# A transformer-like chain of eight stages on one core: norms moved to other engines, three MLP parts and some clearing moved in time

## The chip, the cores and the metric

The kernel runs on one core of a Trainium2 chip. A core has a matrix engine (TensorE, in the profile PE, with its weight loads listed apart as PEld) and three engines for the rest: VectorE (DVE), ScalarE (ACT) and GpSimd (POOL). Every engine takes its instructions in a fixed order and waits on semaphores for the others. SyncE (SP) issues most plain DMAs, and POOL issues the gathers and scatters whose addresses are data. The metric is the device time of one execution in microseconds (us). The kernel is measured over several runs and the median counts; the profile comes from one further execution.

## The reference, cut to what matters

There are 8192 tokens of 128 features, 32 sequences of 256. Four layers follow one another, and each has an attention half and a feed-forward half, all of one form:

```
h = _layernorm(x) * (1 + ca) + sa
x = x + ga * attention(h, ...)
h = _layernorm(x) * (1 + cb) + sb
x = x + gb * feed_forward(h, ...)
```

The halves that the change touches are these.

```
# layer 0, feed-forward: a shared MLP and 8 experts, two chosen per token
shared = new_gelu(xf @ Wfc_s + bfc_s) @ Wproj_s + bproj_s
probs = softmax(xf @ Wr);  topk_p, topk_i = top_k(probs, 2)      # renormalized
routed = sum_e gate[:, e] * (new_gelu(xf @ Wfc[e] + bfc[e]) @ Wproj[e] + bproj[e])
return shared + routed

# layer 1, feed-forward: 8 experts with a capacity of 512 token copies
logits = relu(x @ rw1 + rb1) @ rw2 + rb2
vals, ids = top_k(logits, 2);  probs = softmax(vals)
pos = cumsum(one_hot(ids)) - 1;  keep = pos < CAP
disp[ids, pos] += x * keep                                        # 8 x 512 rows
eo = relu(disp @ ew1 + eb1) @ ew2 + eb2
y = eo[ids, pos] * probs * keep

# layer 3, attention: 16 heads of 8, keys and values from a latent of 32
q = x @ Wq + bq
latent = x @ Wl + bl
k = latent @ Wk + bk;  v = latent @ Wv + bv
out = (softmax(q k^T * 8 ** -0.5) v) @ Wo + bo
```

The layer norm has no weights here; it needs the mean, the variance and 1 / sqrt(variance + 1e-5) of each token. Between the two routed halves lies the attention of layer 1 (called hale in the code), and behind the latent attention an MLP with four-bit rounding of its operands (fp4_mlp).

## The kernel before

The residual stream x stays in on-chip memory as 16 blocks, each 128 features by 512 tokens. The eight halves run one after the other. In the profiled execution the first routing (`dense_moe`) takes 1107 to 1376 us, its 39 expert blocks 1376 to 1682, `hale` 1682 to 3731, the second routing (`capacity_moe`) 3731 to 4000 and its experts to 4085, `phase_attention` 4085 to 4790, `head_moe` to 5545, `latent_attention` 5545 to 6400 and what is left of `fp4_mlp` to 6648.

**Order.** Each stage fills an agenda: `put(t, f)` places a piece of work in slot t, and then all slots are gone through in order. Within a slot, work is done in the order in which it was put there. The instructions of an engine are issued in this order; a flag (`strict`) keeps them in program order where a scheduler could change it. So an agenda slot fixes a place in the queue of every engine that the work uses, and a waiting instruction holds back everything behind it on its engine.

**First routing.** Token block b has T = 4b: statistics in slot T, norm in T + 1, the modulated h in T + 3, router logits and the choice of two in T + 5, slot numbers and the scatter of token rows to per-expert regions in DRAM in T + 10 (POOL, eight scatters of 128 rows), gates in T + 13, and the shared MLP in T + 24 to T + 27 (`shared_part`, L1117: four matmuls to 512 hidden features, each with a gelu on ACT, then one for the bias and four for the outputs, and the residual on DVE). In slot 72 the totals are formed, and 39 expert blocks follow, four slots apart: `block_fetch` gathers weights and 4 x 128 rows by POOL, `block_turn` transposes them, `block_hidden` and `block_out` multiply, and the results go to DRAM. Block j has its first matmuls in slot 4 (23 + j) = 92 + 4j and its last in slot 99 + 4j.

**hale.** At its start POOL waits for the last expert rows, clears the tiles for maxima (`mts`), for values (`vzb`, `vzl`) and for key states (`kvs`), and then runs eight gathers per token block (`gather_rows`), which DVE sums up, weighted, into the residual of the routed experts. These are side works from slot 32 b - 62 on for token block b, in this stage's own count.

**Second routing.** Again T = 4b: `norm_stats` (L417) leaves the turned rows in PSUM and mean and variance in SBUF; `norm_apply` (L435) makes the root and the normed rows; `norm_out` modulates; `router_hidden` has four matmuls with relus, `router_sums` the logits, `router_choice` the choice of two (`choose`, L1051, with the running counts `both` and `past`), and `capacity_slots` positions and scatters. The root is taken on DVE by `newton_parts` (L960): two integer operations and four Newton steps, which is 14 operations of 128x4. In the trace they stand between those of the choice of two.

**Latent attention.** Per token block there are 16 score groups, eight for each of two sequences; each has maxima (`max_step`, DVE reduces a score tile), scores again with the maxima taken off, exponentials (`exp_step`, ACT) and weighted values. `before(b)` puts the preparation of a block around its first slot: statistics at -14 (`norm_rows`, L446, copies the turned rows to SBUF and takes statistics), the root and the normed rows at -13 and -12 (`norm_place`, L462: DVE), h at -10, latent at -8, q at -6, keys at -4 (`keys`, L1548), values at -2. The keys are kept twice, masked for even and odd heads; ACT writes the four masked copies straight from the score buffer S in PSUM, with the bias and a row of ones (for the maxima) added by the same instruction. The front of the last stage runs ahead in here too, one token block behind: `mlp_norm` and the rest of `mlp_front`, four slots from its norm to its h. Only token block 15's front is left for the last stage.

Of the kernel before, what the change touches and what calls it, by code (L numbers as in the profile page):

```python
# [24 lines left out]
AF = mybir.ActivationFunctionType  # L25
ALU = mybir.AluOpType
# [4 lines left out]
P = 128  # L31
NSEQ, SEQ = 32, 256
NB = 16
TB = 512
# [106 lines left out]


def rows(v):

    v = np.asarray(v, np.float32).reshape(1, -1)
    return np.broadcast_to(v, (P, v.shape[1]))
# [29 lines left out]
def packs(d):  # L176
# [91 lines left out]
    k.add("Wl", g["Wl"])  # L268
    k.add("Wk", spread(g["Wk"]))
    k.add("Wo", gathered(g["Wo"]))  # L270
    k.add("Wv", np.concatenate([g["Wv"], g["bv"][None]], 0))
    k.add("bq", spread(g["bq"][None])[0].T)
    k.add("kb", key_bias(g["bk"]))
    k.add("bo", col(g["bo"]))
# [41 lines left out]
class Program:  # L316
# [129 lines left out]
    def norm_rows(self, src, small=None, tag="ln_xn"):  # L446
# [13 lines left out]
        return xn, mv, v  # L460

    def norm_place(self, xn, mv, v):  # L462

        rs = self.wk("ln_rs", (P, 4))
        yield from self.newton_parts(rs, v, "ln")
        for n in range(4):
            self.nc.vector.tensor_scalar(
                xn[:, n, :], xn[:, n, :], mv[:, n, 0:1], rs[:, n : n + 1], ALU.subtract, ALU.mult
            )
        yield  # L470
# [7 lines left out]

    def norm_newton(self, mv, v, r):


        pool = self.nc.gpsimd
        t = self.wk("ln_t", (P, 4))
        pool.tensor_tensor(t, r, r, ALU.mult)
        pool.tensor_tensor(t, t, v, ALU.mult)
        pool.tensor_scalar(t, t, -0.5, 1.5, ALU.mult, ALU.add)
        pool.tensor_tensor(r, r, t, ALU.mult)
        shift = self.wk("ln_m", (P, 4))
        pool.tensor_tensor(shift, mv[:, :, 0], r, ALU.mult)
        pool.tensor_scalar(shift, shift, -1.0, None, ALU.mult)  # L490
        return r, shift

    def norm_scale(self, xn, r, shift):
# [482 lines left out]
    def dense_moe(self, w):  # L976
# [8 lines left out]
        with ExitStack() as ctx:  # L985
# [19 lines left out]
            def put(t, f, *args):  # L1005
                agenda.setdefault(t, []).append((f, args))

            for b in range(NB):
                a = {"b": b}
                T = 4 * b  # L1010
                put(T + 1, lambda a: a.update(xn=self.norm_apply(*a["st"])), a)
                put(T + 0, lambda a: a.update(st=self.norm_stats(self.x[a["b"]])), a)
                put(T + 3, lambda a: a.update(h=self.norm_out(a["xn"], self.ada_mods(0, 1, a["b"]), "h")), a)
                put(T + 5, self.route_logits, m, a)
                put(T + 10, self.route_slots, m, a)
                put(T + 13, self.route_gates, m, a)
                for i in range(4):
                    put(T + 24 + i, self.shared_part, m, a, i)
            end = 4 * NB + 8
# [528 lines left out]
    def keys(self, h, w, bias):  # L1548
# [14 lines left out]
        return k4  # L1563


    def hale(self, w):
        nc, c = self.nc, self.c
        BF = mybir.dt.bfloat16
        with ExitStack() as ctx:
# [8 lines left out]
            self.vzl = [keep.tile([P, 4, 16, 32], F, name=f"vzl{t}") for t in (0, 1)]  # L1578
            for t in self.mts + self.vzb + self.vzl:
                nc.gpsimd.memset(t, 0.0)  # L1580
            for t in self.vzb + self.vzl:
                nc.gpsimd.memset(t[:, :, :, 8:16], 1.0)
            self.identb = wk("identb", (P, P), BF)
# [4 lines left out]
            self.kvs = wk("kvs", (P, 5, SEQ))  # L1588
            nc.gpsimd.memset(self.kvs, 0.0)
            self.kt = wk("kt", (P, 5, P))  # L1590
# [19 lines left out]
            self.gather = None  # L1610

    def hale_slots(self, w):

# [6 lines left out]

        tiles = {}
        for q in range(2 * NB):
            b, s = divmod(q, 2)
# [402 lines left out]
    def capacity_moe(self, w):  # L2026
# [3 lines left out]
        with ExitStack() as ctx:  # L2030
# [6 lines left out]
            self.pools(ctx, {"tp": 2, "hid": 3, "o": 1, "s": 2}, zero=1, ht=4, dk=4, hid=3, eo=3, h=3)  # L2037
            self.strict = self.newton = True
            zero = self.wk("zero", (P, 8 * P))
# [14 lines left out]
            for b in range(NB):  # L2054
                a = {"b": b}
                T = 4 * b
                put(T + 1, lambda a: a.update(xn=self.norm_apply(*a["st"])), a)
                put(T + 0, lambda a: a.update(st=self.norm_stats(self.x[a["b"]])), a)
                put(T + 3, lambda a: a.update(h=self.norm_out(a["xn"], self.ada_mods(1, 1, a["b"]), "h")), a)
                put(T + 5, self.router_hidden, m, a, 0)  # L2060
                put(T + 6, self.router_hidden, m, a, 1)
                put(T + 8, self.router_sums, m, a)
                put(T + 10, self.router_choice, m, a)
                put(T + 12, self.capacity_slots, m, a)
# [9 lines left out]
            for t in sorted(agenda):  # L2074
                for f, args in agenda[t]:
                    f(*args)
            self.strict = self.newton = False
            self.gather = {"eo": eo, "rows": 8 * CAP}
# [390 lines left out]
    def latent_attention(self, w):  # L2469
        nc, c = self.nc, self.c  # L2470
        self.mlp_start()
        with ExitStack() as ctx:
# [7 lines left out]
            def before(b, tiles):  # L2480
                t = tiles[b] = {"vz": self.vzs[4 * (b % 2) : 4 * (b % 2) + 4]}

                def head():
                    t["st"] = self.norm_rows(self.x[b])
                    t["norm"] = self.norm_place(*t["st"])

# [16 lines left out]
                def k():  # L2503
                    t["k4"] = self.keys(t["lat"][:32, :], w.Wk, w.kb)

# [100 lines left out]
    def mlp_norm(self, a):  # L2606
        a["st"] = self.norm_rows(self.x[a["b"]], tag="fx")
        a["norm"] = self.norm_place(*a["st"])

# [212 lines left out]
```

## Time and profile before

| | us |
|---|---|
| median of 10 runs | 6653.41 |
| lowest and highest run | 6627.98, 6663.11 |
| the profiled execution's own time | 6649.74 |
| span from its first to its last instruction | 6647.3 |
| PE busy in the span | 5819.3 (88%) |
| DVE busy | 4316.2 (65%) |
| ACT busy | 3493.0 (53%) |
| POOL busy | 2660.8 (40%) |
| mean granted clock of TensorE | 0.936 |

The busy shares are means over eight stages with different limits, so the page of the whole kernel says little about one stage. The table of stretches gives busy time and granted clock for a chosen window, and the timeline gives single instructions with the idle time ahead of each and what ended it. In a line of the timeline stand: start, duration, engine, source line, operation, the tiles written and read, the shape, the count, and in brackets the idle time with its releaser. Line L304 is a helper through which DVE's instructions of the later stages are issued, and L392, L396 and L399 are helpers for matmuls, transposes and activations; there one goes by the tile names.

### The profile page before, as it was taken

To read this page: it belongs to the slowest core of one execution; us is meant where nothing else is said; L and a number is where in the kernel's file an instruction comes from. 1 tells how busy PE (TensorE), PEld (TensorE's weight loads), DVE (VectorE), ACT (ScalarE), POOL (GpSimd) and SP (SyncE) were. 2 spreads that over 40 slices of the span, in tenths; PEclk is the share of its full clock that TensorE was granted. 3 is DMA by queue.
4 is the path that set the end of the run, shared out by engine and by line. 5 is a ranking of instruction groups with operands and counts; after the bars stand their busy time and mean duration, and the time that the engine had idled before them with its cause. 6 is when DMAs were issued, how large, how long until landed. Compare 5 with 4: busy or idle time off the path is not lost. (4 is left out here: it accounts for less than half of the span.)

```text
span 6647.3 us, 132969 instructions
## 1 busy us (share of the span) xinstructions
PE 5819.3 (88%) x54369; PEld 3292.5 (50%) x54369; DVE 4316.2 (65%) x9937; ACT 3493.0 (53%) x5026; POOL 2660.8 (40%) x2882
## 2 busy tenths in 40 slices
PE   6788886989899999999999767999799998999986
PEld 4555554456455555555555434555422223444443
DVE  4777776611466666666665553888677774777779
ACT  5888884333344444444444332444388885554532
POOL 3555553565444544544544452444245452000000
PEclk8999997899899999999999778999899998998989
DMA  1110110134000000000000101111044341000011
GB/s 62 42 42 29 42 42 34 37 114 131 22 6 5 7 6 5 7 6 5 7 2 2 47 1 38 27 28 28 29 96 92 90 93 41 17 18 18 17 33 30
DMA packets 175877, 232.19 MB, mean 35 GB/s; under 512 B 46567, under 2 KB 95967, under 8 KB 175010
## 3 DMA queue, kind: packets, MB, share of 16 engines
q1 hardware_dynamic: 124880, 126.50, 7.5%
q0 software_dynamic: 26992, 56.62, 3.4%
q10 hardware_dynamic: 23394, 40.58, 1.6%
q8 instruction: 426, 6.98, 0.4%
q14 instruction: 185, 1.52, 0.1%
HBM read 88.22 MB, written 74.97 MB: 25 GB/s over the span
## 5 line engine op out<-in xcount | busy, mean ns | idle before, releaser
L304 DVE TENSOR_REDUCE mt<-S 128x4 f32<-128x1024 f32 (+2 forms) x768 | 756.0, 999 | 514.0 <-PE S L392 510.8
L1438 ACT ACTIVATE E<-S 128x1024 f32<-128x1024 f32 x448 | 458.9, 1024 | 546.2 <-PE S L392 507.0
L875 DVE TENSOR_TENSOR_SCAN hs<-decay,dB 128x512 f32<-128x512 f32 x512 | 583.0, 1204 | 91.8 <-PE dB L392 77.2
L399 ACT ACTIVATE hid<-S,bigw 128x1024 f32<-128x1024 f32 x512 | 537.4, 1112 | 121.2 <-PE S L392 121.0
L1912 POOL TENSOR_SCALAR_AFFINE_SELECT E<-E 128x1024 f32<-128x1024 f32 x320 | 349.4, 1094 | 583.8 <-ACT E L1911 583.3
L304 DVE TENSOR_TENSOR E<-S,cst 128x1024 f32<-128x1024 f32 x320 | 391.3, 1223 | 288.9 <-PE S L392 287.3
L392 PE MATMUL S<-qa,kx 32*128 32x256 f32 x4096 | 538.5, 382 | 34.4 <-DVE mt L304 34.0
L392 PE MATMUL S<-kx,q 32*128 32x512 f32 (+1 forms) x2048 | 527.8, 610 | 17.0 <-ACT kx L1556 16.1
L1911 ACT COPY E<-S 128x1024 f32<-128x1024 f32 x320 | 323.6, 1011 | 326.0 <-PE S L392 314.1
L2459 POOL TENSOR_TENSOR acc<-acc,ye 128x512 f32<-128x512 f32 x256 | 344.7, 1347 | 359.0 <-DVE ye L304 316.3
L392 PEld LDWEIGHTS S<-qa,kx 32*128 32x128 f32 x4096 | 340.7, 190 | 142.7 <-DVE mt L304 106.7
L392 PE MATMUL S<-qG,f 32*128 32x512 f32 x2560 | 367.6, 644 | 47.5 <-DVE E L304 47.5
L392 PE MATMUL S<-hm,bigw 32*128 32x512 f32 x2048 | 336.8, 649 | 25.2 <-ACT hid L399 25.2
L399 ACT ACTIVATE hsT<-hT 128x1024 f32<-128x1024 f32 x256 | 260.9, 1019 | 157.1 <-PE hT L396 156.2
L399 ACT ACTIVATE decay<-dl,A 128x510 f32<-128x510 f32 x512 | 339.1, 714 | 0.0
L396 PE MATMUL hT<-cst,hs 128*128 128x128 f32 x2048 | 295.7, 290 | 22.6 <-ACT hsT L399 21.5
L392 PE MATMUL po<-hid,bigw 128*32 128x512 f32 x2048 | 277.9, 615 | 30.1 <-DVE ye L304 30.1
L392 PE MATMUL po<-E,vz 128*32 128x256 f32 x4096 | 294.2, 372 | 0.3 <-ACT oc L1458 0.2
L1787 ACT ACTIVATE E<-S 128x768 f32<-128x768 f32 (+1 forms) x192 | 169.2, 881 | 237.9 <-PE S L392 237.9
L304 DVE TENSOR_TENSOR ye<-po,gb 128x512 f32<-128x512 f32 x256 | 176.0, 687 | 173.4 <-PE po L392 106.4
L392 PE MATMUL po<-E,vzl 128*32 128x128 f32 x8192 | 276.7, 276 | 0.0
L396 PEld LDWEIGHTS hT<-cst,hs 128*128 128x128 f32 x2048 | 235.1, 147 | 82.5 <-ACT hsT L399 65.0
(530 smaller groups left out, 12931.6 us busy)
## 6 DMA issues: line engine op xcount, KB each, us to landing
gb<-gT SPq DMA_DIRECT2D x256, 256.0 KB
regions<-zeros ACTq DMA_DIRECT2D x16, 2048.0 KB
rx<-far SPq DMA_DIRECT2D x64, 256.0 KB
expert_rows<-eo SPq DMA_DIRECT2D x39, 256.0 KB
xin<-in_x SPq DMA_DIRECT2D x16, 256.0 KB
out<-out SPq DMA_DIRECT2D x16, 256.0 KB
xTd<-xT SPq DMA_DIRECT2D x15, 256.0 KB
xT<-xTd SPq DMA_DIRECT2D x15, 256.0 KB
```

The source lines that it names most:

```text
L304: return lambda *args, **kw: self.tc.keep_in_program_order(op(*args, **kw))
L392: return self.tc.keep_in_program_order(self.nc.tensor.matmul(out, lhsT, rhs, start=start, stop=stop, **kw))
L396: return self.tc.keep_in_program_order(self.nc.tensor.transpose(out, in_, self.c.ident[:k, :k]))
L399: ins = self.nc.scalar.activation(*args, **kw)
L875: nc.vector.tensor_tensor_scan(hs[:, :, n], decay, dB[:, :, n], 0.0, ALU.mult, ALU.add)
L1438: nc.scalar.activation(e, src, AF.Exp, scale=scale)
L1787: nc.scalar.activation(e, src, AF.Exp, scale=1.0 / math.sqrt(8))
L1911: nc.scalar.copy(e, src)
L1912: nc.gpsimd.affine_select(e, e, [[0, 8], [1, P]], ALU.is_ge, 0.0, base=0, channel_multiplier=-1)
L2459: nc.gpsimd.tensor_tensor(a["acc"], a["acc"], ye, ALU.add)
```

## The change

It has four parts.

1. In the first routing the shared MLP of token blocks 9, 10 and 11 leaves its slots (60 to 71) and goes to slots 252 to 263, behind the last expert block, whose last outputs are in slot 251.
2. At hale's start the clearing leaves its place ahead of the stage and becomes a side work (`hale_zeros`) in slot -47, behind the eight gathers of the first token block (-62 to -50).
3. In the second routing the root is taken by ACT (logarithm, then the exponential of minus half of it) with one Newton step of four operations on DVE, and ACT instead of DVE writes the normed rows, from PSUM, with scale and bias. A table that holds both functions is loaded at the stage's start.
4. In latent attention, and in the part of the last stage's front that runs there, the root comes from ACT in the same way, and POOL does the variance's offset, the Newton step and the normed rows (`norm_apart`). The keys' bias becomes a 33rd row of the key weights; ACT copies the key tile to SBUF once, and POOL makes the masked copies from it, in two multiplications by the mask (`masked_keys`).

```diff
+    def norm_turned(self, ps, mv, v):
+        nc = self.nc
+        rs, shift = self.wk("ln_rs", (P, 4)), self.wk("ln_m", (P, 4))
+        self.rsqrt(rs, v, "ln")
+        nc.vector.scalar_tensor_tensor(shift, mv[:, :, 0], -1.0, rs, ALU.mult, ALU.mult)
+        xn = self.wk("ln_xn", (P, 4, P))
+        for n in range(4):
+            self.act(xn[:, n, :], ps[:, n, :], AF.Identity, bias=shift[:, n : n + 1], scale=rs[:, n : n + 1])
+        return xn
...
+    def norm_apart(self, xn, mv, v):
+        r = self.norm_roots(v)
+        yield
+        r, _ = self.norm_newton(mv, v, r, False)
+        for n in range(4):
+            self.nc.gpsimd.tensor_scalar(
+                xn[:, n, :], xn[:, n, :], mv[:, n, 0:1], r[:, n : n + 1], ALU.subtract, ALU.mult
+            )
+        yield
...
+                last = 4 * (8 + blocks + b + 7) if 9 <= b < 12 else T + 24
                 for i in range(4):
-                    put(T + 24 + i, self.shared_part, m, a, i)
+                    put(last + i, self.shared_part, m, a, i)
...
+    def masked_keys(self, lat, w):
+        pk = self.ps("S", (P, 2, TB))
+        for x in (0, 1):
+            self.mm(pk[:, x, :], w[:, x, :], lat)
+        both = self.wk("kk", (P, 2, TB))
+        self.nc.scalar.copy(both, pk)
+        k4 = self.wk("kx", (P, 2, 2, TB))
+        for x in (0, 1):
+            self.nc.gpsimd.tensor_tensor(
+                k4[:, x],
+                both[:, x, :].unsqueeze(1).to_broadcast([P, 2, TB]),
+                self.c.half.unsqueeze(2).to_broadcast([P, 2, TB]),
+                ALU.mult,
+            )
+        return k4
...
-            for t in self.mts + self.vzb + self.vzl:
-                nc.gpsimd.memset(t, 0.0)
-            for t in self.vzb + self.vzl:
-                nc.gpsimd.memset(t[:, :, :, 8:16], 1.0)
...
-            nc.gpsimd.memset(self.kvs, 0.0)
...
+        put(side, -47, self.hale_zeros)
...
-            self.strict = self.newton = True
+            self.strict = True
+            self.use_ln_exp()
...
-                put(T + 1, lambda a: a.update(xn=self.norm_apply(*a["st"])), a)
+                put(T + 1, lambda a: a.update(xn=self.norm_turned(*a["st"])), a)
...
-                    t["st"] = self.norm_rows(self.x[b])
-                    t["norm"] = self.norm_place(*t["st"])
+                    t["st"] = self.norm_rows(self.x[b], nc.gpsimd)
+                    t["norm"] = self.norm_apart(*t["st"])
...
-                    t["k4"] = self.keys(t["lat"][:32, :], w.Wk, w.kb)
+                    t["k4"] = self.masked_keys(t["lat"], w.Wk)
...
-        a["st"] = self.norm_rows(self.x[a["b"]], tag="fx")
-        a["norm"] = self.norm_place(*a["st"])
+        a["st"] = self.norm_rows(self.x[a["b"]], self.nc.gpsimd, "fx")
+        a["norm"] = self.norm_apart(*a["st"])
```

## The prediction

> **What bounds the kernel now.** I read the table of stretches first (columns: us; busy us and instructions of PE, PEld, DVE, ACT, POOL; granted clock; DMA share; GB/s), cut at the stages that the change touches.
>
> ```profile
> 1107.00:1376.00 269.00, 218.04 (x718) 114.65 (x719) 147.31 (x920) 71.03 (x127) 147.44 (x162) 0.80 0.13 42
> 1376.00:1682.00 306.00, 305.02 (x1715) 213.66 (x1716) 53.19 (x77) 107.24 (x156) 174.90 (x176) 1.00 0.46 127
> ...
> 3731.00:4000.00 269.00, 168.00 (x583) 84.76 (x583) 150.90 (x1029) 83.94 (x146) 131.31 (x150) 0.71 0.12 34
> ...
> 5640.00:6400.00 760.00, 700.27 (x5574) 355.24 (x5573) 554.26 (x1375) 387.18 (x488) 6.20 (x12) 0.94 0.06 19
> 6400.00:6648.00 248.00, 179.23 (x627) 102.09 (x625) 223.03 (x295) 69.91 (x134) 0.00 (x0) 0.89 0.11 32
> ```
>
> First routing (row 1) and second routing (row 3) have no full engine: they are chains of latencies. The expert blocks (row 2) are PE's alone, 305 of 306 us. Latent attention (row 4) is nearly PE's: 60 us idle, and a clock of 0.94. The last stage (row 5) is DVE's, 223 of 248. POOL is empty in rows 4 and 5.
>
> Then the timeline at the end of the first routing, PE only:
>
> ```profile
> 1329.36 3.60 PE L392 MATMUL hid<-h,w 128*128 128x512 f32 x8
> 1332.89 1.12 PE L392 MATMUL o<-gT,w 9*128 9x512 f32 x2
> 1333.94 3.70 PE L392 MATMUL o<-hid,w 128*128 128x512 f32 x8
> 1337.47 3.60 PE L392 MATMUL hid<-h,w 128*128 128x512 f32 x8
> ...
> 1364.84 2.08 PE L392 MATMUL hid<-h,w 128*128 128x512 f32 x2 [15.43 <-ACT hid L399]
> ...
> 1374.27 0.60 PE L396 MATMUL tp<-cst,dk 128*128 128x128 f32 x4
> ```
>
> One shared part costs PE 1337.47 − 1329.36 = 8.1 us. The last one sits in a standstill of 15.4 us while POOL issues the first blocks' gathers; block 0 begins at 1374.27. The next stage's start, on all engines:
>
> ```profile
> 1680.88 0.69 DVE L1257 COPY eo<-o 128x512 f32<-128x512 f32 x1 [4.12 <-PE o L392]
> ...
> 1684.01 1.32 POOL L1580 MEMSET mt<- 128x256 f32 x4 [21.41 <-DMA expert_rows<-eo]
> ...
> 1693.37 1.01 POOL L1266 DMA_INDIRECT got<-expert_rows,back  x1 [0.16 <-issue]
> ...
> 1706.10 0.88 DVE L539 SCALAR_TENSOR_TENSOR x<-tp,mods,x 128x256 f32<-128x256 f32 x2 [0.57 <-PE tp L396]
> ```
>
> The gathers start 12.5 us after the last block: 3.1 us until its rows land, 9.4 us of clearing. The second routing's DVE, within one block's choice:
>
> ```profile
> 3875.53 1.36 DVE L441 TENSOR_SCALAR ln_xn<-tp,ln_mv,ln_rs 128x128 f32<-128x128 f32 x4
> 3876.83 0.19 DVE L588 TENSOR_TENSOR rt_o<-rt_t,rt_f 128x32 f32<-128x32 f32 x1
> ```
>
> The next block's norm (1.36 us) stands between two links of this block's top-2 chain. Last, latent attention: a timeline, another, the table of waits, and a tile of phase attention.
>
> ```profile
> 6136.16 0.88 DVE L304 SCALAR_TENSOR_TENSOR x<-y,mods,x 128x256 f32<-128x256 f32 x2 [1.26 <-ACT y L2524]
> ...
> 6138.14 1.11 DVE L304 TENSOR_SCALAR ln_xn<-ln_xn,ln_mv,ln_rs 128x128 f32<-128x128 f32 x4
> 6139.17 1.22 DVE L304 TENSOR_REDUCE mt<-S 128x4 f32<-128x1024 f32 x1
> ...
> 6140.44 1.48 PE L392 MATMUL S<-qa,kx 32*128 32x256 f32 x8 [1.39 <-DVE mt L304]
> ```
>
> ```profile
> 5652.64 0.92 PE L392 MATMUL S<-kx,q 32*128 32x512 f32 x2 [1.07 <-ACT kx L1556]
> ```
>
> ```profile
> PE S L392 <- DVE mt L304: 30.3, 37, 1.4
> ...
> PE S L392 <- ACT kx L1556: 14.0, 13, 1.1
> ```
>
> ```profile
> L304 DVE TENSOR_TENSOR ga<-ga,gr x14: 100/1488/1559, 4221.9 to 4742.1; 128x8 f32<-128x8 f32 x14
> ```
>
> Both PE waits come once per token block: one for row maxima (mt) that DVE brings late because residual and norm stand before them, one while ACT makes the masked keys (kx) from a score buffer.
>
> **The change, part by part.** Its sum starts from the profiled execution, 6649.74 us; the median of the runs, 6653.41, is 3.7 above it.
>
> *Shared parts behind the blocks, clearing behind the gathers.* 3 × 8.1 = 24.3 us of PE work (with 12 gelus on ACT and 6 residual halves on DVE) leave the routing's end and return after the last block. In the changed order the first gather of the next stage waits for the last matmul of the moved parts, since its tile lies on their memory. So counted from the last block, gathers start at about 24.6 us where they started at 12.5: +12.1. Neither move carries a DMA, and SP's queue keeps its order. The clearing (9.4 us) falls behind eight gathers (8 × 1.31 us, up to the residual at 12.7 us); the block that needs the cleared tiles comes later, so 0, or up to 4 if DVE's second block of sums waits for its gathers. Against this stands how much earlier block 0 begins. From 1321 to 1338 PE is busy throughout, so parts 12 to 15 slide forward; their start is bounded by block 15's routing chain, which I read as 8 to 10 us earlier without shared parts between its links. POOL's scatters (8 × 1.28 us per token block, back to back) let the first fetch start 5 us earlier at most. If the standstill goes with the move, block 0 begins near 1345 (28 earlier); if the gathers bring it back on the same engines, near 1364 (10 earlier); if the routing's pace does not react at all, 0. I take 16, nearer to the case with the standstill, because its cause, the gathers, stays. Net −4, from −16 to +12.
>
> *Second routing.* DVE loses 14 small operations (they fill gaps of a chain whose links come each 0.22 us) and the four norm rows, 1.36 us inside the chain. ACT gets a Ln, an Exp (0.20 each, the row of its 128x4 exponential) and four 128x128 rows, between 0.20 and 0.56 us each (its 128x4 and 128x256 rows): 1.5. One Newton step stays on DVE and waits for that Exp, behind a 0.69-us relu: I charge the chain 0.3. So the place where PE next waits for `both` comes 1.36 us earlier, or 2.0 if the 0.65 us of DVE idle ahead of the second rt_f goes too; I take 1.7 less 0.3 = 1.4, over 13 blocks of about 14.4 us (the last ones go at POOL's 10.2) = −18; the one new table load is 1.28 (as that before the softmax at 1687.37): −17. Bounds: 0, if ACT's order brings the norm as late as DVE did, and 13 × 1.9 = −25.
>
> *Latent attention, norms.* Per norm DVE loses 14 operations of 0.16 and four of 0.34, about 3.8 us with the variance; two norms per token block, 7.6 of 50 us. Their new road: POOL 0.23, ACT 0.4, POOL 4 × 0.2 and four 128x128 scalings. POOL has no such row; its 128x4 (0.23) and 128x512 (1.76) give 0.60 between them by width, its 128x128 copy 0.36, so 1.5 to 2.4 us. In sum 3.8 us against four agenda slots of 3.1 us, so hidden. *Keys:* four ACT rows of 0.78 become one copy, 1.01 us (row `COPY E<-S`), and two POOL products at 1.89 (row `qG<-f,cst`): the score buffer is free 1.8 us earlier, the keys are ready 1.7 us later, in four slots that are hidden.
> What goes: the maxima come 2.1 us earlier (6139.17 against 6137.04), over the 1.39 wait; the buffer 1.8 earlier, over the 1.07. 15 × (1.39 + 1.07) = 37 us. What is late next is the residual behind ACT's y (1.26 us of DVE idle), so I keep three quarters: −28. The granted clock drops to 0.50 behind these waits (5851 to 5861, for one); such dips add up to about 92 us in the clock's records of this stage, 46 us lost. Other breaks in PE's work share in them: I take back 40%, −18. Latent −46, from 0 to −83.
>
> The Trainium skill, "TensorE: Matmul & The Clock Gate" (Part 1, the HAM clock gate), has only half and full rate, judged over about 3.4 us; dips of 3.4, 6.8 and 10.2 us here agree. By it a 1.1-us gap alone need not cost a dip, and the estimate would be −28 for this stage.
>
> Against the change speaks the last row: a 128x8 product on DVE takes 1.49 us beside a busy POOL, where its short ones take 0.10. Latent attention's POOL would hold about 2 × 3.4 + 3.8 = 10.6 of 50 us; four DVE operations per block (`oT`, `x`) of the kind would meet it one time in five: 4 × 0.21 × 1.4 = 1.2 us of DVE, less than the 7.6 freed. The skill's "SBUF — State Buffer" (Who interferes with whom) says that a DVE operation with two SBUF inputs waits out a GpSimd one that reads SBUF, and a reduction never; by it the maxima stay untouched, which would leave the sum as it is.
>
> *Last stage.* One norm remains in it: DVE −3.8, ACT three table loads of 1.28 in order. Between −4 and +4: 0.
>
> Sum: −4 − 17 − 46 + 0 = −67: 6649.7 − 67 = 6583 for an execution, 6586 beside the median.
>
> **Rivals.**
> - *Half the gain:* the freed waits of latent attention re-form at `y` and at ACT's exponentials (PE must still alternate with them), and the dips stay: −10 there, 0 to −5 for the shared parts: −4 − 17 − 10 = −31, 6622. For it: PE is at 92% already. Against: phase attention runs the same skeleton at a clock of 0.99.
> - *No change:* block 0 begins no earlier (+12), the second routing meets POOL or ACT order (−5), latent −10: 6650.
> - *Slower, one mechanism:* POOL brings the norms late. Decisive is a norm that takes over 12.4 us; 3.8 of its own, 3.8 of keys ahead of it and ACT's queue (1.03 per exponential, two or three) come to 11. Past that each block misses by whole slots: one is 3.1 × 15 = +46 us, against −21 for the maxima, dips kept: latent +25, and 6650 − 4 − 17 + 25 = 6654, still the same time. It decides from the second slot on, 6654 + 46 = 6700; I price the rival between them and that, 6680. Against: POOL is empty.
>
> **How the numbers follow.** Forecast 0.50, half the gain 0.24, no change 0.12, slower 0.14. About 0.2% (13 us) is what a measurement of this kernel can tell from none. Half the gain at 6622 is faster too: 0.74 faster, 0.12 same, 0.14 slower. The forecast's own range puts each term halfway to its bounds: −10 − 21 − 64 = −95 and +4 − 9 − 23 = −28, so 6555 to 6622. The full range starts at 6540, most of the way to all gain bounds together (−16 − 25 − 83 − 4 = −128, 6522, hardly all at once), and ends at 6662, which takes in no change and leaves out most of the slower case.
>
> **What would show it.** Right: first gather 24 us after the last block and block 0 near 1358; routing period near 13 us; 5640-6400 stretch near 715 us at a clock over 0.96, no 1.39 or 1.07 waits, POOL near 160 us busy. Wrong: block 0 still at 1370, PE waiting for ACT's ln_xn in the routing, or PE waiting for POOL's kx or for h in latent attention.

## The result and the profile after

The changed kernel takes 6595.01 us (median of 9 runs, 6578.35 to 6605.19) against 6647.33 us for the kernel before over all its 31 runs. The ratio is 0.9917, with a 95% interval of 0.9905 to 0.9929, so 52 us are gone by the two medians and 55 by the ratio. The forecast was 6586. The profiled execution of the changed kernel has a span of 6595.4 us, 51.9 less than that of the kernel before.

The sum came out close, but the terms did not. Read from the two timelines by the same events in both, the stages changed so: from the start to the last expert block's copy −9.6 us; from there to the second routing's first statistics +26.3; from those to the first gather of its experts' results +4.2; phase attention and the head MLPs, which no part of the change touches, +11.2; latent attention −82.0; the last stage −2.1. So one part gave more than all the others cost.

The stretches after, cut at the same events (columns: from and to; us; busy us and instructions of PE, PEld, DVE, ACT, POOL; granted clock; DMA share; GB/s):

```profile
1106.00:1356.00 250.00, 196.17 (x660) 107.83 (x661) 142.83 (x911) 63.38 (x115) 144.47 (x159) 0.77 0.13 44
1356.00:1671.00 315.00, 307.85 (x1716) 214.63 (x1715) 54.04 (x79) 107.19 (x156) 178.04 (x179) 0.99 0.45 123
...
3751.00:4021.00 270.00, 161.01 (x581) 80.43 (x582) 114.00 (x807) 106.68 (x243) 124.56 (x128) 0.73 0.11 31
...
5672.00:6350.00 678.00, 653.29 (x5571) 335.55 (x5566) 462.30 (x841) 369.00 (x501) 174.88 (x292) 0.99 0.07 21
6350.00:6595.00 245.00, 181.74 (x627) 102.31 (x625) 220.07 (x276) 73.70 (x139) 8.77 (x9) 0.88 0.11 33
```

Row 4 is latent attention, 678 us where it was 760. Two things changed in it: PE's idle time fell from 60 to 25 us, and PE's busy time fell from 700 to 653 us for the same matmuls, mostly because the granted clock rose from 0.94 to 0.99: by the trace's clock records 49 us of the stretch were lost to half clock before and 9 after. DVE fell by 92 us, and POOL, which had 6 us of work, has 175. Row 3 is the second routing: DVE lost 37 us of work and ACT gained 23, and the stretch is as long as before.

The start of hale, on the changed kernel's timeline:

```profile
1671.33 0.69 DVE L1290 COPY eo<-o 128x512 f32<-128x512 f32 x1 [4.12 <-PE o L398]
...
1696.39 1.00 POOL L1299 DMA_INDIRECT got<-expert_rows,back  x1 [43.36 <-PE o L398]
...
1707.55 1.09 POOL L1660 MEMSET mt<- 128x256 f32 x4
1707.79 8.77 DVE L310 TENSOR_SCALAR gy<-got,pair 128x128 f32<-128x128 f32 x1 [0.89 <-DMA got<-expert_rows,back]
...
1715.45 1.01 POOL L1662 MEMSET vzl<- 128x512 f32 x2
...
1717.53 0.88 DVE L569 SCALAR_TENSOR_TENSOR x<-tp,mods,x 128x256 f32<-128x256 f32 x2 [0.57 <-PE tp L402]
```

POOL waits 43 us for the last matmul of the moved shared parts, and its first gather comes 25.1 us after the last block's copy (12.5 before). The clearing does run behind eight gathers. But the last weighted product of the first token block, 0.28 to 0.35 us elsewhere, takes 8.77 us: it begins with the clearing and ends 0.1 us after it. The first residual stands 46.2 us behind the last block's copy, where it stood 25.2.

### The profile page after: what moved, and what is told of

Its sections match the earlier page's. It is cut to its first block, busy times and chain, and to the rows that moved or that the text cites. A ratio compares the mean times of both kernels' runs of the same rounds, so it can differ in the third digit from the quotient of the medians.

```text
span 6595.4 us, 132502 instructions
## 1 busy us (share of the span) xinstructions
PE 5792.1 (88%) x54369; PEld 3280.7 (50%) x54369; DVE 4185.1 (63%) x9121; ACT 3499.1 (53%) x5142; POOL 2852.3 (43%) x3202
## 5 line engine op out<-in xcount | busy, mean ns | idle before, releaser
L398 PE MATMUL S<-qa,kx 32*128 32x256 f32 x4096 | 512.0, 372 | 11.7 <-DVE mt L310 11.1
L398 PE MATMUL S<-kx,q 32*128 32x512 f32 (+1 forms) x2048 | 514.6, 596 | 3.0 <-POOL kx L1607 2.7
L398 PEld LDWEIGHTS S<-qa,kx 32*128 32x128 f32 x4096 | 326.6, 185 | 96.9 <-DVE mt L310 64.1
L398 PE MATMUL S<-hm,bigw 32*128 32x512 f32 x2048 | 340.9, 655 | 25.2 <-ACT hid L405 25.2
L402 PE MATMUL hT<-cst,hs 128*128 128x128 f32 x2048 | 296.7, 291 | 21.6 <-ACT hsT L405 20.4
```

Source lines behind the costliest of these rows:

```text
L398: return self.tc.keep_in_program_order(self.nc.tensor.matmul(out, lhsT, rhs, start=start, stop=stop, **kw))
L402: return self.tc.keep_in_program_order(self.nc.tensor.transpose(out, in_, self.c.ident[:k, :k]))
```

## The experiments

Each run also measured the kernel before on the same chip, and ratios are against that. Chips differ: the kernel before took 6632.52, 6649.38 and 6574.40 us in the three groups of runs.

Single executions differ too. The last expert block's copy lies at 1668 to 1678 us in nine profiles of the first two groups and of the changed kernel, at 1649 in all four of the third group, and at 1680.9 in the profile of before on which the forecast was built. Stretches that are the same in all kernels vary by several us: from the layer-1 expert results' first gather to the last head-MLP sum 1469 to 1484 us (1472.1 before, 1483.3 changed). So a part is judged below by the distance between events at its own place, over several profiles.

**Shared parts back beside the routing.**

```diff
-                last = 4 * (8 + blocks + b + 7) if 9 <= b < 12 else T + 24
+                last = T + 24
```

> The changed kernel with the three shared parts back beside the first routing (clearing still behind the first gathers). Theory (each part's own place): block 0 starts about 9.6 us later, but the first gather no longer waits for 24.6 us of matmuls: it comes 3.4 us after the last block, so about 12 us earlier than in the changed kernel; the 8.8-us hold of one DVE product beside the clearing stays. Whole kernel about 12 us below the changed one, ratio to the kernel before about 0.990. Rival (the move pays): first gather later than in the changed kernel, ratio 0.993 or more.

Measured: 6561.11 us, ratio 0.990 [0.988, 0.9921]. The first gather is 3.8 us after the last block's copy instead of 25.1, and the first row maxima of hale come 38.3 us after it instead of 60.6. The last block's copy is at 1670.1; the changed kernel had it at 1671.3. So the theory holds for the gather and is wrong in the other half: block 0 may start earlier when the parts move, but the block phase does not end earlier.

The same loss is seen on the third group's chip, too: there the first maxima come 60.6 us after the last block's copy with the move (skip_rows) and 38.3 us without (two_parts), both described below.

Why the move does not shorten the blocks is seen best on the third group's chip. There the moved parts let block 0 begin at 1333.06 us (skip_rows, which has the move) instead of 1339.64 (two_parts, which has not), and the last block's copy is at 1649.6 against 1648.8. First the timeline of the kernel with the moved parts, then that of the other:

```profile
1333.06 0.60 PE L402 MATMUL tp<-cst,dk 128*128 128x128 f32 x4
...
1363.63 2.08 PE L398 MATMUL hid<-dT,wts 128*128 128x512 f32 x2 [7.79 <-DMA wts<-in_s1e,idx_wi]
...
1370.01 0.60 PE L402 MATMUL tp<-cst,dk 128*128 128x128 f32 x4
```

```profile
1339.64 0.60 PE L402 MATMUL tp<-cst,dk 128*128 128x128 f32 x4
...
1364.73 1.13 PE L398 MATMUL hid<-dT,wts 128*128 128x512 f32 x2 [2.32 <-DMA wts<-in_s1e,idx_wi]
...
1369.20 0.60 PE L402 MATMUL tp<-cst,dk 128*128 128x128 f32 x4
```

The fourth block waits for its weights, 7.8 us with the move and 2.3 without, and the fifth block begins at 1370.0 and 1369.2: whatever block 0 gained is waited out there. On the other chips the same happens earlier. The standstill during the first gathers lasts to about 1362 us or longer whatever is queued on PE: in the changed kernel PE waits 7.04 us for block 0's turned rows, in route_back (below) 13.63, and multiplies them from 1364.6 and 1361.9 us on. Without the move it does so from 1363.5 (share_back) and 1362.9 us (latent_alone, below).

**Clearing back ahead of the gathers.**

```diff
             self.vzl = [keep.tile([P, 4, 16, 32], F, name=f"vzl{t}") for t in (0, 1)]
+            for t in self.mts + self.vzb + self.vzl:
+                nc.gpsimd.memset(t, 0.0)
+            for t in self.vzb + self.vzl:
+                nc.gpsimd.memset(t[:, :, :, 8:16], 1.0)
...
+            nc.gpsimd.memset(self.kvs, 0.0)
...
-        put(side, -47, self.hale_zeros)
```

> The changed kernel with the clearing back ahead of hale's gathers. Theory (the clearing is not hidden, it holds a DVE product for 8.8 us): first gather 9.4 us later, no long DVE product, first residual within 1 us of the changed kernel's 1717.5; ratio equal to the changed kernel's, 0.992. Rival (the clearing was hidden and the long product is something else, for instance a late gather): residual 9 us later, ratio 0.993 to 0.994, and the 8.8-us product still there.

Measured: 6591.63 us, ratio 0.9944 [0.9924, 0.9964]. The first gather comes 33.8 us after the last block's copy (25.1 changed), no DVE product is long, and the first residual is at 1717.1 us (1717.5 changed). The theory holds at its place: the 9 us that the clearing gave POOL were paid by DVE. The ratio lies at the rival's number, but no event of this stage goes with it: the first maxima follow the last block's copy by 59.8 us here and by 59.3 to 60.6 us in the kernels with both moves. With the shared parts back, too, it is 38.3 us with the clearing moved (share_back) and 39.7 without (latent_alone, next but one). But two_parts and dk_two, both with the clearing moved, have 38.3 and 39.6, so what the move is worth cannot be told from nothing.

**The second routing's norm on DVE again.**

```diff
-            self.strict = True
-            self.use_ln_exp()
+            self.strict = self.newton = True
...
-                put(T + 1, lambda a: a.update(xn=self.norm_turned(*a["st"])), a)
+                put(T + 1, lambda a: a.update(xn=self.norm_apply(*a["st"])), a)
```

> The changed kernel with the second routing's norm on DVE again. Theory (the routing's mean period is set by something other than the DVE chain, the scatters): slot numbers of the first and the last token block lie 204 to 212 us apart with either norm (206.0 before, 210.8 changed), so within 5 us of the changed kernel. Rival 1 (ACT's order costs the routing): 5 us or more faster than the changed kernel. Rival 2 (the norm does help and this one execution hid it): 10 us or more slower, over 215 us.

Measured: 6579.22 us, ratio 0.9915 [0.9892, 0.9939]. From the first to the last slot numbers 206.7 us, against 210.8 in the changed kernel. That is the theory's range, but the sign is the same in every profile with eight scatters outside the third group: 206.0, 206.7 and 206.5 us with DVE's norm (before, this, latent_alone), and 210.8, 211.1, 212.9, 215.8 and 215.2 with ACT's. Within the first group ACT's norm costs 4 to 6 us over this distance, which speaks for rival 1. The pattern differs too: with ACT's norm, periods of 9, 21 and 13 us follow one another; with DVE's most are 13 to 15. In one of the long periods of the changed kernel everything stands still (timeline, one line each for DVE, ACT and PE):

```profile
3896.49 0.89 DVE L434 BATCH_NORM_STATS2 ln_st<-tp 128x6 f32<-128x128 f32 x4 [5.56 <-remote]
...
3899.33 0.69 ACT L405 ACTIVATE hid<-hid,bigw 128x512 f32<-128x512 f32 x1 [6.51 <-remote]
...
3900.07 2.07 PE L398 MATMUL hid<-h,bigw 128*128 128x512 f32 x2 [9.78 <-ACT hid L405]
```

Both ACT and DVE waited for something that the trace calls remote, while POOL issued scatters back to back (from 3888.6 to 3898.5, eight of them). Outside the third group, DVE has one such wait of 5 us or more per routing with DVE's norm (before, this, latent_alone) and three to five with ACT's. So ACT's norm goes together with more standstills; why is not shown.

A second cost lies ahead of the first slot numbers. ACT's first work in this stage is held by DMAs that ACT issues itself. First the changed kernel's ACT, then this one's:

```profile
3766.19 0.21 ACT L405 ACTIVATE ln_t<-ln_v 128x4 f32<-128x4 f32 x1 [6.54 <-DMA disp<-zero]
...
3769.73 1.02 ACT L405 ACTIVATE h<-tp,mods 128x256 f32<-128x256 f32 x2 [0.57 <-PE tp L402]
```

```profile
3762.45 1.02 ACT L405 ACTIVATE h<-tp,mods 128x256 f32<-128x256 f32 x2 [18.92 <-DMA disp<-zero]
```

DVE has its normed rows ready by then, and ACT goes straight to h; ACT's own root and rows only begin there, and h comes 3.5 us later. From the first statistics to the first h it is 17.7 and 18.1 us with DVE's norm (this, latent_alone), 21.5 and 21.6 with ACT's (share_back, clear_back). Over the whole stage, from the first statistics to the first gather of its experts' results, these kernels take 350.8 and 350.7 against 359.4 and 361.1 us: within this group ACT's norm costs 9 to 10 us.

**Latent attention's part alone**, that is, share_back, clear_back and route_back together.

> The kernel before with the latent attention's part of the change alone (norms and keys). Theory: latent attention 83 us shorter and all else as before: 6647 - 83 - 2 = 6562, ratio 0.987. Rival (phase attention and head MLPs lose 13 us because of the change, as the two traces show side by side): their stretch 4211 to 5577 of the changed kernel's clock is 12 us longer here too, ratio 0.989. Rival 2 (the 83 us are this execution's luck): ratio 0.992 or more.

Measured: 6557.57 us, ratio 0.9895 [0.9874, 0.9917]. From the last head-MLP sum to the last attention output it takes 761.0 us, against 844.2 before and 762.2 in the changed kernel. The stretch of phase attention and head MLPs is 1478.6 us, between before's and the changed kernel's, and two_parts (below), which has latent attention's change too, takes 1469.4. That speaks against the rival: its 13 us vary by execution.

**Only the keys, or only the norms, back in latent attention.** In keys_back the keys are made by ACT from PSUM with the packed bias; in norms_back DVE takes roots and scales rows.

```diff
-                    t["k4"] = self.masked_keys(t["lat"], w.Wk)
+                    t["k4"] = self.keys(t["lat"][:32, :], w.Wk, w.kb)
```

> The changed kernel with the keys masked by ACT from the score buffer again (norms still apart). Theory (two waits, each with its own part): the 1.07-us wait for kx comes back once per token block, 16 us, with part of the half-clock dips, 10 to 25 us in all: the stretch from the last head-MLP sum to the last attention output goes from 762 us to 772 to 787. Rival (the keys did nothing, DVE's relief did it all): within 4 us of 762. Rival 2 (either wait alone brings back all the dips): over 800.

```diff
-                    t["st"] = self.norm_rows(self.x[b], nc.gpsimd)
-                    t["norm"] = self.norm_apart(*t["st"])
+                    t["st"] = self.norm_rows(self.x[b])
+                    t["norm"] = self.norm_place(*t["st"])
...
-        a["st"] = self.norm_rows(self.x[a["b"]], self.nc.gpsimd, "fx")
-        a["norm"] = self.norm_apart(*a["st"])
+        a["st"] = self.norm_rows(self.x[a["b"]], tag="fx")
+        a["norm"] = self.norm_place(*a["st"])
```

> The changed kernel with latent attention's and the last stage's norms on DVE again (keys still by ACT and POOL). Theory: the 1.39-us wait for the maxima comes back, 21 us, with most of the half-clock dips, 40 to 65 us in all: 762 becomes 802 to 827, and the last stage is 2 us longer. Rival (the keys are the larger part): 762 becomes less than 790.

Measured: keys_back 6596.01 us, ratio 0.9913 [0.9884, 0.9943], and 765.7 us for the stage; norms_back 6659.89 us, ratio 1.0013 [0.9996, 1.0031], and 830.5 us. The norms are nearly all of it: 68 us with the keys already moved, 78 without (keys_back against before). The whole times of the two runs, on one chip, say the same: 64 us apart. The keys are worth 13.7 us without the norms moved, by one execution of each kernel. With the norms moved nothing is shown: kernels whose latent attention is just the changed one's take 761 to 766 us (latent_alone, two_parts), and keys_back's 765.7 lies among them. So the keys' theory was too high, its first rival's range holds, and the norms' range was just too low. The inner stretch of this stage, before, changed, norms_back and keys_back:

```profile
5673.00:6387.00 714.00, 664.10 (x5315) 336.36 (x5313) 529.69 (x1325) 369.45 (x465) 5.69 (x11) 0.94 0.06 18
```

```profile
5705.00:6337.00 632.00, 615.55 (x5277) 316.71 (x5277) 436.49 (x797) 350.19 (x477) 166.47 (x280) 1.00 0.06 21
```

```profile
5688.00:6388.00 700.00, 662.00 (x5314) 331.18 (x5310) 528.16 (x1328) 347.99 (x426) 54.36 (x37) 0.96 0.06 19
```

```profile
5700.00:6336.00 636.00, 605.59 (x5252) 316.55 (x5255) 435.99 (x795) 370.12 (x514) 117.93 (x254) 1.00 0.06 20
```

With the norms on DVE the clock is 0.96 and PE busy 662 us; with them away 1.00 and 616. PE's busy time makes 46 us of the difference, and its idle time, 38 against 16.5 us, the other 21. By the trace's clock records the four stretches lose 41, 3, 29 and 3 us to half clock, so the clock explains 26 us of the 46; what the other 20 are is not shown. Moving the keys alone takes PE's idle time from 50 to 38 us and the clock's loss from 41 to 29, and leaves PE's busy time. The table of waits (us in total, times, longest) goes with it; of norms_back, of the changed kernel, and of keys_back, where the wait for the keys is back:

```profile
PE S L398 <- DVE mt L310: 30.0, 37, 1.4
```

```profile
PE S L398 <- DVE mt L310: 10.4, 23, 1.0
```

```profile
PE S L399 <- ACT kx L1590: 12.9, 12, 1.1
```

**Half of the second routing's scatters**, with the norm on ACT and on DVE (only the first choice's rows are written).

```diff
-            for k in (0, 1):
+            for k in (0, 1) if rows != 8 * CAP else (0,):
```

> The changed kernel with only the first choice's rows scattered in the second routing (the second choice's rows stay zero, so that part of the result is left out): four scatters per token block instead of eight. Theory (the scatters set the routing's mean period, in pairs of 9 us and one of 21 us): the long periods vanish, and the period falls to the chain's own, about 11 to 12.5 us; first to last slot numbers 165 to 190 us instead of 210.8. Rival (the long periods come from the chain or from something unrelated to scatters): 200 us or more, long periods still there.

> The same with half of the scatters, and the second routing's norm on DVE again. Theory: without the scatters' limit the norm's price is seen: 1.4 us per token block longer than with ACT's norm, 15 to 25 us over the routing. Rival (ACT's norm is no shorter a chain): equal to it within 5 us or faster.

Measured: 6485.88 us, ratio 0.9752 [0.9704, 0.98], and 6527.09 us, 0.9814 [0.9767, 0.9861]. First to last slot numbers take 125.0 and 152.5 us. These are the stretches of the routing in half_new, in half_old and in the changed kernel:

```profile
3779.00:3904.00 125.00, 111.05 (x502) 55.90 (x500) 101.45 (x740) 88.72 (x204) 58.44 (x60) 0.97 0.02 3
```

```profile
3791.00:3944.00 153.00, 125.99 (x505) 63.10 (x503) 126.68 (x910) 72.06 (x127) 58.45 (x60) 0.87 0.02 3
```

```profile
3788.00:3998.00 210.00, 137.25 (x501) 68.34 (x499) 102.84 (x734) 89.12 (x204) 114.35 (x118) 0.77 0.02 4
```

With half of the scatters the period is 8.4 to 8.5 us up to the last two, the long ones are gone, PE is at 0.97 of its clock, and the norm by ACT is worth 27.5 us, 1.8 per token block. So the chain did get shorter, as forecast (1.4), and more than the theory's 11 to 12.5 us allowed; with eight scatters per token block something behind them sets the pace.

**Scatters without rows** (all eight issued, the second choice's four with a bound that excludes nearly every row).

```diff
-                    bounds_check=rows - 1,
+                    bounds_check=0 if k and rows == 8 * CAP else rows - 1,
```

> The changed kernel with all eight scatters per token block issued in the second routing, but with the bound of the second choice's four set so that no row is within it and none is written (the second choice's part of the result is left out). Theory A (issuing and describing a scatter is what limits): as the changed kernel, first to last slot numbers 205 to 216 us. Theory B (moving the rows limits): as with four scatters, 125 to 150 us.

Measured: 6500.30 us, ratio 0.9886 [0.9867, 0.9906]; 145.3 us. The period is 8.6 to 8.8 us at first and then 10.2, eight scatters at POOL's 1.28. That is theory B's number, but the run fell on the chip where the kernel two_parts, with all rows and DVE's norm, takes 170.9 us, with most periods at 11.5 to 12.5, and has no standstills. With full rows and ACT's norm nothing was measured on that chip, so moving rows is not shown to be the limit; that issuing alone does not need 13 us is shown.

**A version without the two losing parts**: shared parts and routing norm as before, clearing and latent attention as changed.

> The changed kernel with the three shared parts back beside the first routing and the second routing's norm on DVE again: of the change it keeps latent attention and the clearing behind the first gathers. Theory (the shared parts cost about 20 us before hale's first maxima, ACT's norm costs 4 to 9 in the second routing, the clearing is worth 1 to 3): 25 to 32 us below the changed kernel, ratio to the kernel before 0.987 to 0.990. Rival (the pieces do not add): 0.9917, the changed kernel's.

Measured: 6492.49 us, ratio 0.9872 [0.9856, 0.9889]. It beats the changed kernel (0.9917), and the intervals do not meet. That compares ratios from different chips, and this chip is not the one on which ACT's norm was shown to lose, so what the second routing's part is worth there is open; the 21 us of the shared parts were seen on both.

**The first weighted products by ACT** (on two_parts, for the first token block only).

```diff
+            if b == 0 and self.gather["rows"] != 8 * CAP:
+                nc.scalar.activation(y[:, t, :], got[:, 0, :], AF.Copy, scale=self.pair[:, 0, at])
+            else:
                 nc.vector.tensor_scalar(y[:, t, :], got[:, 0, :], self.pair[:, 0, at], None, ALU.mult)
```

> The kernel two_parts, with the first of the two weighted products of hale's first token block (four of 128x128) made by ACT instead of DVE. Theory (POOL's run of memsets holds a DVE product with one tensor from on-chip memory, not one with two): no DVE instruction over 3 us beside the memsets, first residual 8 us earlier after the last block's copy (17 us instead of 24.8); first maxima up to 8 us earlier, less if the norm's small DVE operations are held next. Rival (DVE is held by the last gather, or any DVE operation is held): the next weighted product takes the 8 us, the residual stays at 24.8.

Measured: 6494.73 us, ratio 0.9878 [0.9862, 0.9895], so no gain over two_parts. At its place the theory holds. DVE beside the clearing, which runs from 1663.4 to 1672.3 us here:

```profile
1665.07 0.35 DVE L310 SCALAR_TENSOR_TENSOR gy<-got,pair,gy 128x128 f32<-128x128 f32 x1 [2.24 <-DMA got<-expert_rows,back]
1665.99 0.88 DVE L569 SCALAR_TENSOR_TENSOR x<-tp,mods,x 128x256 f32<-128x256 f32 x2 [0.57 <-PE tp L402]
...
1668.89 3.45 DVE L438 TENSOR_SCALAR ln_v<-ln_mv 128x4 f32<-128x4 f32 x1
```

The product with two tensors takes its 0.35 us in the middle of the clearing, and the residual comes 17.5 us after the last block's copy instead of 24.8. Then the norm's 128x4 TENSOR_SCALAR, 0.17 us in the changed kernel, is held for 3.45 us, to the clearing's end. The first maxima come 4 us earlier than in two_parts, and the sixteenth 3 us later. That sixteenth one lies 79.0 us (two_parts) or 88.3 us (dk_two) after the last block's copy in kernels that are alike there, so what becomes of the 4 us cannot be told.

**Two buffers for gathered rows instead of four** (on two_parts).

```diff
-                h=9, gT=9, at=1, wts=3, dk=4, hid=3, ht=3, eo=3, idx=1,
+                h=9, gT=9, at=1, wts=3, dk=2, hid=3, ht=3, eo=3, idx=1,
```

> The kernel two_parts with two buffers instead of four for the expert blocks' gathered rows, so that POOL issues 8 instead of 16 of these gathers in a row before block 0. Theory (the standstill ahead of the blocks lasts as long as POOL issues gathers back to back): block 0's turned rows 8 to 10 us earlier (about 1352), the last block's copy near 1660 instead of 1668 to 1671. Rival (the standstill has another cause, or the blocks need the lead of four): last block's copy at 1667 or later.

Measured: 6498.91 us, ratio 0.9885 [0.9868, 0.9901]; the last block's copy at 1648.7 (1648.8 in two_parts). There is no standstill on this chip with either number of buffers, so the question is not answered.

## Why the prediction was right or wrong

*The sum.* 6586 forecast, 6595 measured. The forecast's terms were −4, −17, −46 and 0. By the distances at their own places they are about +21, +9 to +10, −82 and −2, which makes −54 to −53 against a measured −52 to −55. That 6586 came so near is luck: the first two terms were each some 25 us too favourable, and the third was 36 us too small.

*Shared parts and clearing, forecast −4 between −16 and +12: wrong, outside its range.* The +12.1 us from the last block to the first gather were right (25.1 against 12.5). Two other steps failed. "I take 16" for the earlier start of block 0 should have been 0: on neither chip that had both did the last block's copy come earlier (1670.5 and 1668.4 us with the move, 1670.1 and 1667.8 without; 1649.6 and 1648.8 in the third group), and the 9.6 us between the two first profiles are most of all the late copy in the profile of before, 1680.9. The first blocks are paced by gathers of weights and rows, not by PE, so what is taken from PE ahead of them is waited out. The stretches had shown PE full in the block phase as a whole, not in its first 30 us. And the clearing "falls behind eight gathers" at "0, or up to 4" held a DVE product for 8.8, so that the first residual came 21 us later and not 12.1. The row that could have told it was in the profile of before: beside the clearing at hale's start the softmax's 128x4 TENSOR_SCALARs took 1.03 and 1.37 us there; after, without the clearing beside them, 0.27 and 0.23.

*Second routing, forecast −17, from −25 to 0: wrong in sign.* The chain's step was right, 1.8 us per block where 1.4 was forecast, once half of the scatters are left out. What failed is "over 13 blocks of about 14.4 us": the forecast took this period for the DVE chain's because POOL's issue needs only 10.2 us. The period is set behind the issue, by what is not shown. A sign of it was in the kernel before: its periods were 10.0 and then 21.8 us at one place, 14.0 at others, which no chain of fixed length makes. The sum also lacked the 3.5 us at the stage's start, where ACT's root and rows wait behind ACT's own DMAs.

*Latent attention, forecast −46 in 0 to −83: direction and mechanism right, size at the bound.* PE's wait for the keys went, and its waits for the maxima fell from 30.3 to 10.4 us (the prediction priced one long wait per token block; its table counts 37 waits in 13 blocks). The residual's wait for y, which was to be late next (22.3 us of DVE idle before, 33.1 after), holds back little: PE's idle time fell by 35 us of the 37. Mis-sized is the clock's term, 18 us of 46: by the clock records some 40 came back. The split between keys and norms shows which wait the dips followed: the 1.39 us before the maxima rather than the 1.07 before the keys. Gaps of up to 1.1 us, one per token block (keys_back), leave the clock at 1.00. The estimate by the clock's rule alone, −28, was further off: where the longest waits for the maxima are 1.4 us (norms_back) the stretch loses 29 us to half clock. Whether their length or what else DVE does late around them matters was not tried.

*The costs on the new road.* POOL's 128x128 scaling takes 0.79 us, not 0.36 to 0.60, so a norm's way is 5.1 us (5799.89 to 5804.96, the four scalings in one line) instead of 3.8; it is still within its four slots.

```profile
5799.89 0.23 POOL L465 TENSOR_SCALAR ln_v<-ln_mv 128x4 f32<-128x4 f32 x1 [8.29 <-DVE ln_mv L310]
...
5801.83 3.13 POOL L518 TENSOR_SCALAR fx<-fx,ln_mv,ln_rs 128x128 f32<-128x128 f32 x4
```

POOL was busy 175 us (160 forecast). The feared meeting of DVE with POOL cost nothing in latent attention: `oT`, with two on-chip tensors, never ran beside a POOL instruction in the changed kernel (0 of 32). The residual `x`, also with two, did so 13 times, beside POOL's scalings, and took 0.483 to 0.486 us where it takes 0.476 to 0.486 alone. The meeting that did cost time was at hale's start, where I had not looked for it.

*Last stage, forecast 0:* −2.1, and −2.0 in norms_back too, so it is not the norm's.

*The rivals.* "Slower" needed a late norm, and none was. "No change" was nearer than the forecast on the shared parts (+12) and had the routing's sign wrong (−5); "half the gain" kept the forecast's −4 and −17. Both had latent attention at −10, which is wrong.

## What to carry to other kernels

A stage that repeats may look like one engine's chain and still be paced by something else, here something behind its scatters. Before pricing a shorter chain, look whether the periods scatter (9, 21, 13 us) where a chain would repeat, and leave out half of the transfers to see the chain's own period. Work that is taken from the engine which is full over a phase helps only if that engine is full at the phase's start, too. When an engine with 1.4-us waits shows half clock in the same stage, the waits may be worth three times their length: here 20 us less of waits for the maxima (30.0 to 10.4) went with 64 to 68 us of time.

## What the runs showed of the hardware

A DVE TENSOR_SCALAR from on-chip memory to on-chip memory stood still until POOL's whole run of 13 memsets was over, not for one of them: 8.64 to 8.77 us instead of 0.28 in all ten profiles where the product meets the clearing, and 3.45 us for a 128x4 one that came in the middle. A SCALAR_TENSOR_TENSOR with two such inputs ran at 0.35 us beside the same memsets. The Trainium skill, "SBUF — State Buffer" (Who interferes with whom), has a port pair that tensor_scalar can take in its fast modes and that only one of DVE and GpSimd holds, each for a whole instruction, and has a two-input DVE operation contend only with GpSimd reads; the second half agrees with the 0.35 us beside memsets, and the hold over 13 instructions is longer than its words say.

In the second routing ACT and DVE stood still for 5 to 14 us at a time under scatters issued back to back, at 13.7 to 14.4 us per eight scatters in two groups of runs and in the profiles of before and of the changed kernel, while on a third chip the same scatters (with DVE's norm) went at 11.4 us in the mean, without standstills. What holds the engines is not settled.
